# A graph layer's edge rows: one chunk in fifty-nine fetched row by row on the sync queue, destinations made relative in PSUM, the index load behind a clear

## The chip, the cores and the metric

The kernel runs on one core of a Trainium2 chip. The metric is device time in microseconds, the median of several executions. The core has TensorE (matmuls; PE in the profile, its weight loads PEld), VectorE (DVE), ScalarE (ACT), GpSimd (POOL) and SyncE (SP). Each has its own instruction queue and they meet at semaphores. SP, ACT and POOL also issue DMA transfers, which 16 DMA engines carry out.

## The reference

One pre-norm graph layer over N = 12500 nodes of D = 128 features and E = 200000 edges. `dst` comes sorted.

```python
src = src[_o]; dst = dst[_o]              # _o = argsort(dst)
h = jnp.maximum(_layernorm(x, axis=-1), 0.0)
# the layer, with z = h
msgs = z[src]
agg = jax.ops.segment_sum(msgs, dst, num_segments=n)
deg = jax.ops.segment_sum(jnp.ones((src.shape[0],), z.dtype), dst, num_segments=n)
agg = agg / jnp.maximum(deg, 1.0)[:, None]
h = jax.nn.relu(agg @ Wg + z @ Ws + bg)
h = jnp.tanh(h @ W1 + b1)                 # 128 -> 512
h = jnp.tanh(h @ W2 + b2)                 # 512 -> 512
return x + h @ W3 + b3                    # 512 -> 128
```

## The kernel before

The edges are cut into 1563 chunks of 128, the nodes into 28 blocks, 24 of them of 512 nodes. Since `dst` is sorted, chunk c falls into a window of 144 nodes around node 8c (88 and 56 near the end). A chunk's messages are added by one matmul: 128 gathered rows times a one-hot matrix of the edges' places in the window.

**Setup.** `rsrc` and `rdst`, the indices of 80 "raw" chunks, are loaded first on SP (L105 to L109). GpSimd makes four ramps with iota and then gathers the raw chunks' rows straight from `x` (L124); these are normalized later. Meanwhile SP loads `x` in pieces, VectorE and ScalarE normalize them (L153 to L165) and SP stores them to the table `htab` in memory (L206). `indices` (L169) loads all of `src` or `dst` as 98 rows of 2048 on ScalarE's queue, clears only the last two rows first (L171), casts to float (L178), turns it with 16 TensorE transposes (L184) and copies the result from PSUM (L185): into `scol`, the row numbers for the gathers, and `dloc`, the destinations. Then `low`, the first node of each chunk's window, is built from two ramps (L211) and taken off `dloc` (L218, L220).

**Main loop** (L521). For chunk c: every eighth chunk VectorE makes the one-hots of the group two further on (`onehot`, L294) and counts them (L312); then `gather` (L267) issues one indirect DMA on GpSimd for each chunk up to AHEAD = 32 chunks ahead, into one of 32 buffers; then `add` (L352) issues the chunk's matmul. Where a block's last chunk is in, `layers` (L438) is started; it is a generator, and the loop takes one step of it every second chunk, so its matmuls are woven between the chunks' matmuls. From chunk QUICK = 1376 on, a small planner with due times picks the steps instead (L539 to L544). The last step of a block stores the output from SP (L492, L495). `own` (L400) loads a block's own rows of `x` and `htab` on SP 40 chunks before the block ends. Matmuls, and DMAs of the main loop on SP, are kept in program order. Every SP or ACT transfer counts on one of eight semaphores in turn, and waits there for the transfer eight before it.

After the windowed part a flag tells whether all edges were counted; SP, ACT, POOL, PE and DVE load it into a register (L907). If not, a second, general routine would run. With these inputs it doesn't.

Of the kernel before, what the change touches and what calls it, by code (L numbers as in the profile page):

```python
# [18 lines left out]
F32 = mybir.dt.float32  # L22
BF16 = mybir.dt.bfloat16
I32 = mybir.dt.int32
AF = mybir.ActivationFunctionType
ALU = mybir.AluOpType
AX = mybir.AxisListType
# [2 lines left out]
P = 128  # L30
# [6 lines left out]
RAW0 = 256  # L37
STEP = 40
AHEAD = 32
QUICK = 1376  # L40

WINDOWS = ((0, 144), (1496, 88), (1536, 56))
# [9 lines left out]
def windowed(ctx, tc, x, src, dst, Wg, Ws, bg, W1, b1, W2, b2, W3, b3, out, flag):  # L52
# [20 lines left out]
    def raw(c):  # L73
        return RAW0 <= c < RAW1 and (c - RAW0) % STEP < GRP


    def first(w, span=per):
        return (span - w) // 2

# [12 lines left out]
    dram = ctx.enter_context(tc.tile_pool(name="dram", bufs=1, space=bass.MemoryType.DRAM))  # L92
    const = ctx.enter_context(tc.tile_pool(name="const", bufs=1))
    raws = ctx.enter_context(tc.tile_pool(name="raws", bufs=1))
    rows_in = ctx.enter_context(tc.tile_pool(name="rows_in", bufs=AHEAD))
    ps_c = ctx.enter_context(tc.tile_pool(name="ps_c", bufs=1, space=PSUM))
    ps_a = ctx.enter_context(tc.tile_pool(name="ps_a", bufs=2, space=PSUM))
# [17 lines left out]
    row_i = const.tile([P, NROW], I32, name="row_i")  # L115
    nc.gpsimd.iota(row_i, pattern=[[per * CPR, NROW]], base=0, channel_multiplier=0)
    q_i = const.tile([P, CPR], I32, name="q_i")
    nc.gpsimd.iota(q_i, pattern=[[per, CPR]], base=0, channel_multiplier=0)

    raw_rows = []  # L120
    for g in range(NRAW):
# [13 lines left out]
    nc.vector.memset(eps, EPS)  # L135

    shared = ps_c.tile([P, BLK], F32, name="shared")
    lane = shared[:, :W_MAX]
    stats_raw = shared[:, BLK - 2 * NRAW * GRP :].rearrange("p (s c) -> p s c", s=2)
    assert W_MAX + 2 * NRAW * GRP <= BLK  # L140
    nc.vector.tensor_copy(lane, lane_i)


# [22 lines left out]

    with tc.tile_pool(name="setup", bufs=1) as sp, tc.tile_pool(name="ln", bufs=2) as ln:

        def indices(name, a, col, pad):  # L169
            r = sp.tile([NROW, ROW], I32, name="idx_raw")  # L170
            nc.vector.memset(r[FULL // 32 * 32 :], pad)  # L171
            even = FULL // 16 * 16
            for s0, s1 in ((0, even), (even, FULL)):
                if s1 > s0:
                    nc.scalar.dma_start(r[s0:s1, :], a[s0 * ROW : s1 * ROW].rearrange("(p e) -> p e", e=ROW))
            nc.scalar.dma_start(r[FULL : FULL + 1, :REST], a[FULL * ROW : E].rearrange("(p e) -> p e", p=1))
            rf = sp.tile([NROW, ROW], F32, name="idx_f")
            nc.vector.tensor_copy(rf, r)  # L178

            col3 = col.rearrange("p (r q) -> p r q", q=CPR)  # L180
            for q0 in range(0, CPR, 4):
                p = ps_m.tile([P, 4, P], F32, name="pm")
                for q in range(4):
                    nc.tensor.transpose(p[:, q, :NROW], rf[:, (q0 + q) * P : (q0 + q + 1) * P], ident[:NROW, :NROW])  # L184
                nc.vector.tensor_copy(col3[:, :, q0 : q0 + 4], p[:, :, :NROW].rearrange("p q r -> p r q"))  # L185


        pieces = [(0, 4), (4, PIECE - 4)] + [(t, min(PIECE, NT - t)) for t in range(PIECE, NT, PIECE)]
        for i, (t0, k) in enumerate(pieces):
            xt = ln.tile([P, PIECE, D], F32, name="xt", bufs=3)  # L190
            whole = min(N - t0 * P, k * P) // P
            rest = min(N - t0 * P, k * P) - whole * P
            if rest:
                nc.vector.memset(xt[:, whole, :], 0.0)
            nc.sync.dma_start(xt[:, :whole, :], x[t0 * P : (t0 + whole) * P, :].rearrange("(t p) d -> p t d", p=P))
            if rest:
                nc.sync.dma_start(xt[:rest, whole, :], x[(t0 + whole) * P : N, :])
            if i == 1:
                indices("src", src, scol, 0)
            stats = ps_a.tile([P, BLK], F32, name="agg")[:, : 2 * k].rearrange("p (s t) -> p s t", s=2)  # L200
            xt = xt[:, :k]
            centre(ln, xt, k, stats)
            factors(stats)
            h = ln.tile([P, PIECE, D], F32, name="h")
            scale(h[:, :k], xt, k, stats)
            nc.sync.dma_start(htab[t0 * P : (t0 + k) * P, :].rearrange("(t p) d -> p t d", p=P), h[:, :k])  # L206


        indices("dst", dst, dloc, 2 * N)
        low = sp.tile([P, NROW, CPR], F32, name="low")  # L210
        nc.vector.tensor_tensor(  # L211
            low, row_i[:, :, None].to_broadcast([P, NROW, CPR]), q_i[:, None, :].to_broadcast([P, NROW, CPR]),
            op=ALU.add,
        )
        low = low.rearrange("p r q -> p (r q)")
        for (c0, w), c1 in zip(WINDOWS, [c for c, _ in WINDOWS[1:]] + [NCOL]):
            v = dloc[:, c0:c1]
            nc.vector.scalar_tensor_tensor(v, v, float(-first(w)), low[:, c0:c1], op0=ALU.add, op1=ALU.subtract)  # L218
        steps, at = (t[:, RAW0:RAW1].rearrange("p (u k) -> p u k", k=STEP) for t in (dloc, low))
        nc.vector.scalar_tensor_tensor(  # L220
            steps[:, :, :GRP], rdst, float(-first(W_RAW, per * GRP)), at[:, :, :1].to_broadcast([P, NRAW, GRP]),
            op0=ALU.add, op1=ALU.subtract,
        )


# [38 lines left out]
    def sp_dma(*a):  # L264
        tc.keep_in_program_order(nc.sync.dma_start(*a))

    def gather(c):  # L267
        r = rows_in.tile([P, D], F32, name="rows")
        nc.gpsimd.indirect_dma_start(  # L269
            out=r, out_offset=None, in_=htab,  # L270
            in_offset=bass.IndirectOffsetOnAxis(ap=scol[:, c : c + 1], axis=0),
        )
        rows_t[c] = r

    def raw_stats(i):
        return stats_raw[:, :, i * GRP : (i + 1) * GRP]
# [118 lines left out]
                skip_group_check=True,  # L395
            )

    owns, hTs, xss = {}, {}, {}

    def own(s):  # L400

# [36 lines left out]
    def layers(b):  # L438
# [50 lines left out]
        o = ml.tile([P, BLK // P, D], F32, name="o")  # L489
        if whole:  # L490
            nc.vector.tensor_tensor(o[:, :whole], po[:, :whole], xb[:, :whole], op=ALU.add)
            sp_dma(out[n0 : n0 + whole * P, :].rearrange("(t p) d -> p t d", p=P), o[:, :whole, :])  # L492
        if rest:
            nc.vector.tensor_tensor(o[:rest, whole], po[:rest, whole], xb[:rest, whole], op=ALU.add)
            sp_dma(out[n0 + whole * P : n0 + n, :], o[:rest, whole, :])  # L495

    order = [c for c in range(NCH) if not raw(c)]
    work, done, nxt, behind = [], 0, 0, 0
    ngrp = -(-NCH // GRP)
    span = BLK // per  # L500
    now = 0

    def soonest():
        two = work[: 2 if len(work) > 1 and work[1][3] < work[0][3] else 1]
        return min(two, key=lambda w: max(w[2], now), default=None)

    def go_on(w):
        nonlocal now
        if w:
            now = max(now, w[2]) + w[1]  # L510
            w[1:] = *next(w[0], (None, 0)), w[3] + 1
            w[2] += now
            if w[1] is None:
                work.remove(w)
# [5 lines left out]
    counted = 0  # L520
    for c in range(NCH):  # L521
        g = c // GRP
        if c % GRP == 0 and g + 2 < ngrp:
            onehot(g + 2)
            if raw((g + 2) * GRP):
                raw_scaled(((g + 2) * GRP - RAW0) // STEP)
            if 2 <= g < 2 + NRAW:
                centre(ed, raw_rows[g - 2], GRP, raw_stats(g - 2))
            if g == 2 + NRAW:
                factors(stats_raw)  # L530

        while c % GRP == GRP // 2 and counted < len(blocks) and reach[counted][-1] // GRP <= g + 1:
            count(counted)
            counted += 1
        while nxt < len(order) and nxt < behind + AHEAD:
            gather(order[nxt])
            nxt += 1
        behind += not raw(c)
        if c >= QUICK:  # L539

            there = 12.0 + 1.25 * (NRAW * GRP + order.index(c))
            while soonest() and max(now, soonest()[2]) < there:
                go_on(soonest())
            now = max(now, there) + 0.27  # L544
        add(c)

        if done < len(blocks) and (c - 2 if across[done] else c) == reach[done][-1]:
            if across[done]:
                merge(done)
            work.append([layers(done), 0, 0, 0])  # L550
            done += 1
        if (c // span + 1) * BLK < N:
            if c % span == span - 40:
                own(c // span + 1)
            if c % span == span - 10:
                own_turned(c // span + 1)
        if c < QUICK:
            if c % 2 == 0:
                go_on(work[0] if work else None)
        if c == QUICK:  # L560
            for b, (_, n) in enumerate(blocks):
                if n < BLK:
                    own_part(b)
    while soonest():
        go_on(soonest())
    seen = const.tile([1, 1], F32, name="seen")
    nc.vector.tensor_reduce(seen, total, AX.X, ALU.add)
    nc.vector.tensor_scalar(flag, seen, float(E), None, op0=ALU.not_equal)
# [373 lines left out]
```

## Time and profile before

| What | Value |
|---|---|
| median of 3 runs | 1982.81 us (1982.66 to 1984.70) |
| profiled execution: its time, its span | 1984.11 us, 1982.3 us |
| granted TensorE clock, mean | 0.913 |
| POOL busy, instructions | 1482.4 us (75%), 1571 |
| PE, DVE, ACT busy | 1364.0, 1067.4, 232.3 us |
| gathers on POOL: from the table, raw | 1483, 80 |
| landing of a gather, median | 2.5 us |
| SP's 256 KB loads `xb` and `hb`, landing | 4.5 and 4.9 us, 24 each |
| SP's 256 KB stores of the output, landing | 2.5 us, 23 |
| DMA: moved, mean rate | 139.40 MB, 70 GB/s |

In the profile a group line names line, engine, operation and tiles, then the count, the busy time, the mean of one in ns, and the idle time before it with what ended most of it. A line of the list of waits gives who waited for whom, the total in us, the number of times and the longest. A timeline line gives start and duration in us, then the instruction, and in brackets the idle time before it. An engine name with a small q (SPq, ACTq) is the engine's queue: issuing transfers and loading registers stand there. Most matmuls share line 256 and most of SP's transfers line 265, since small helpers issue them; tiles tell them apart.

### The profile page before, as it was taken

How to read it: one execution, taken by the hardware profiler on the slowest of the kernel's cores; microseconds unless marked ns; L12 is line 12 of the kernel's file. 1: busy time of each engine (PE TensorE's matmuls, PEld its weight loads, DVE VectorE, ACT ScalarE, POOL GpSimd, SP SyncE). 2: the span in 40 equal slices, each digit the busy share in tenths (PEclk: the TensorE clock that was granted, in tenths of full speed). 3: DMA queues.
4: the chain of work that ended last, by engine and by line, in shares of the span. 5: the costliest groups of instructions: out<-in, count | busy, mean ns of one | idle time of the engine just before them, and what ended most of it. 6: DMA issues, size and time to landing. Idle time of an engine off the chain costs nothing.

```text
span 1982.3 us, 15097 instructions
## 1 busy us (share of the span) xinstructions
PE 1364.0 (69%) x5213; PEld 806.2 (41%) x5213; DVE 1067.4 (54%) x650; ACT 232.3 (12%) x364; POOL 1482.4 (75%) x1571
## 2 busy tenths in 40 slices
PE   1046576678778777766676676766767776778797
PEld 1024443344444444433433334333343443444466
DVE  7952884555666556645445445454554544545440
ACT  1100211001111111101011010110110001101122
POOL 7777777777777777777777777777777777777774
PEclk9999889899889989898898988989989889878697
DMA  9722222222222222222222222222222222222221
GB/s 239 198 63 58 53 68 53 69 67 55 69 69 69 56 66 69 68 53 69 68 53 69 52 69 69 52 69 69 53 69 53 68 69 52 69 76 60 56 62 40
DMA packets 120806, 139.40 MB, mean 70 GB/s; under 512 B 30796, under 2 KB 94876, under 8 KB 120526
## 3 DMA queue, kind: packets, MB, share of 16 engines
q0 software_dynamic: 50016, 102.53, 20.7%
q1 hardware_dynamic: 67544, 32.50, 5.9%
q10 hardware_dynamic: 3160, 3.31, 0.6%
q8 instruction: 43, 0.70, 0.2%
q14 instruction: 43, 0.35, 0.1%
HBM read 125.42 MB, written 12.82 MB: 70 GB/s over the span
## 4 chain that ended last, share of the span: by engine, by line
issue 35%; DMA 30%; PE 22%; POOL 11%; DVE 1%; ACT 0%; POOLq 0%; DVEq 0%; SPq 0%; ACTq 0%
DMA rows<-htab,scol 29%; PE pm L256 11%; POOL rows L269 8%; PE agg L256 7%; POOL raw L124 4%; PE edge L256 3%; PE pt L259 1%; DVE oh L302 0%; DMA rsrc<-in_src_dram 0%; DVE shared L158 0%; DVE shared L154 0%; DVE raw L155 0%; ACT sq L157 0%; DVE rd L339 0%; DMA raw<-in_x_dram,rsrc 0%
## 5 line engine op out<-in xcount | busy, mean ns | idle before, releaser
L269 POOL DMA_INDIRECT rows<-htab,scol x1483 | 1401.5, 945 | 451.9 <-issue 302.9
L256 PE MATMUL agg<-oh,rows 128*128 128x144 f32 (+3 forms) x2120 | 549.4, 358 | 364.0 <-DMA rows<-htab,scol 349.2
L256 PEld LDWEIGHTS agg<-oh,rows 128*128 128x128 f32 x2120 | 372.4, 218 | 750.7 <-DMA rows<-htab,scol 605.2
L256 PE MATMUL pm<-h,w 128*128 128x512 f32 (+3 forms) x1344 | 618.7, 556 | 0.4 <-ACT h L460 0.3
L302 DVE TENSOR_TENSOR oh<-shared,dloc 128x1152 f32<-128x1152 f32 (+2 forms) x186 | 244.9, 1322 | 622.8 <-PE agg L256 419.0
L312 DVE TENSOR_REDUCE cnt<-oh 128x200 bf16<-128x1600 f32 (+2 forms) x186 | 522.9, 2824 | 4.5 <-DMA htab<-h 0.4
L256 PE MATMUL edge<-oh,rows 128*128 128x144 f32 (+2 forms) x846 | 220.4, 353 | 146.1 <-DMA rows<-htab,scol 136.2
L256 PEld LDWEIGHTS edge<-oh,rows 128*128 128x128 f32 x846 | 145.4, 211 | 293.2 <-DMA rows<-htab,scol 233.6
L256 PEld LDWEIGHTS pm<-h,w 128*128 128x128 f32 x1344 | 212.5, 196 | 12.0 <-issue 9.6
L476 ACT ACTIVATE h<-pm,b2c 128x512 f32<-128x512 f32 (+3 forms) x112 | 70.9, 633 | 669.1 <-PE pm L256 669.1
L124 POOL DMA_INDIRECT raw<-in_x_dram,rsrc x80 | 80.0, 1000 | 27.9 <-issue 23.5
L467 ACT ACTIVATE h<-pm,b1c 128x512 f32<-128x512 f32 (+3 forms) x112 | 70.3, 633 | 189.5 <-PE pm L256 189.0
L339 DVE RECIPROCAL rd<-rd 128x512 f32<-128x512 f32 (+3 forms) x28 | 81.8, 2920 | 0.0
L453 DVE TENSOR_TENSOR mT<-agg,rd 128x512 f32<-128x512 f32 (+3 forms) x28 | 17.3, 620 | 108.0 <-PE agg L256 108.0
L259 PE MATMUL pt<-ident,hb 128*128 128x128 f32 x98 | 16.7, 297 | 57.2 <-DMA xb<-in_x_dram 57.2
L337 DVE TENSOR_SCALAR rd<-pm 128x512 f32<-128x512 f32 (+3 forms) x28 | 17.4, 621 | 63.8 <-PE pm L256 63.8
L460 ACT ACTIVATE h<-pm,bgc 128x512 f32<-128x512 f32 (+3 forms) x28 | 17.7, 632 | 234.9 <-PE pm L256 234.9
L482 ACT ACTIVATE h<-pm,b3c 128x512 f32<-128x512 f32 (+3 forms) x28 | 17.7, 633 | 187.7 <-PE pm L256 187.7
L256 PE MATMUL pm<-hT,ws 128*128 128x512 f32 (+3 forms) x56 | 37.2, 758 | 0.0
L259 PEld LDWEIGHTS pt<-ident,hb 128*128 128x128 f32 x98 | 13.3, 155 | 57.5 <-issue 57.5
L158 DVE TENSOR_REDUCE shared<-sq 128x8 f32<-128x1024 f32 x10 | 12.2, 1221 | 43.9 <-ACT sq L157 43.9
L424 ACT COPY hT<-pt 128x512 f32<-128x512 f32 (+1 forms) x25 | 14.4, 578 | 156.7 <-PE pt L259 156.7
(64 smaller groups left out, 486.0 us busy)
## 6 DMA issues: line engine op xcount, KB each, us to landing
rows<-htab,scol POOLq DMA_INDIRECT x1483, 2.5
xb<-in_x_dram SPq DMA_DIRECT2D x24, 256.0 KB, 4.5
hb<-htab SPq DMA_DIRECT2D x24, 256.0 KB, 4.9
out_dram<-o SPq DMA_DIRECT2D x23, 256.0 KB, 2.5
htab<-h SPq DMA_DIRECT2D x6, 896.0 KB, 5.8
xt<-in_x_dram SPq DMA_DIRECT2D x5, 896.0 KB, 9.3
raw<-in_x_dram,rsrc POOLq DMA_INDIRECT x80, 4.2
w<-in_L_gnn_W_dram ACTq DMA_DIRECT2D x1, 1024.0 KB, 8.0
```

What stands on the lines that cost most here:

```text
L124: nc.gpsimd.indirect_dma_start(out=t[:, j, :], out_offset=None, in_=x, in_offset=bass.IndirectOffsetOnAxis(ap=rsrc[:, g, j : j + 1], axis=0),)
L256: tc.keep_in_program_order(nc.tensor.matmul(*a, **k))
L259: tc.keep_in_program_order(nc.tensor.transpose(*a, **k))
L269: nc.gpsimd.indirect_dma_start(out=r, out_offset=None, in_=htab, in_offset=bass.IndirectOffsetOnAxis(ap=scol[:, c : c + 1], axis=0),)
L302: nc.vector.tensor_tensor(oh[:, :k, :w], lane[:, None, :w].to_broadcast([P, k, w]), dloc[:, g * GRP : g * GRP + k][:, :, None].to_broadcas ...
L312: nc.vector.tensor_reduce(cnt[:, :n], shifted, AX.X, ALU.add)
L337: nc.vector.tensor_scalar(rd[:, :m], dg[:, :m], 1.0, None, op0=ALU.max)
L339: nc.vector.reciprocal(rd[:, :m], rd[:, :m])
L460: nc.scalar.activation(h0[:, :n], p0[:, :n], AF.Relu, bias=bgc)
L467: nc.scalar.activation(h1[:, m, :n], p1[:, :n], AF.Tanh, bias=b1c[:, m : m + 1])
L476: nc.scalar.activation(h2[:, m, :n], p2[:, :n], AF.Tanh, bias=b2c[:, m : m + 1])
L482: nc.scalar.activation(h3[:, :n], p3[:, :n], AF.Identity, bias=b3c)
```

## The change

1. **Row loads on SP.** Every 59th chunk that isn't raw, from chunk 72 up to QUICK, is taken out of the gathers' order. That is 21 chunks. Their indices come to one partition (`places`), VectorE multiplies them by 512, the bytes of a row, and SP loads 16 of the products at a time into registers and issues 16 transfers of 512 bytes, each from the byte offset in a register to one partition of a tile. There are two such tiles. Each time the loop has passed 58/8 gathered chunks, the next 16 rows are issued, so a chunk takes 58 gathers in the program's order; the first 16 rows stand at chunk 7.
2. **SP's order.** `own` moves from 40 to 52 chunks before a block's end. An output store is noted when its block is done and issued 12 chunks later, up to QUICK; after that at once.
3. **Destinations.** `low` is built before the `dst` load, from a copy of one ramp in PSUM and the other ramp in SBUF, and holds the whole offset of the window; 72 and 32 columns get a further constant. `dst` is then subtracted while it is read out of PSUM, four times for a quarter each.
4. **Index load.** The whole tile (98 x 2048) is cleared instead of two rows, so the load of the first 96 rows waits for it. In the built program the loads of `wg`, `ws`, `w1` and `w2` now stand ahead of it on ScalarE's queue.

```diff
...
+SLOW0 = 72
+EACH = 58
+LOADS = 16
+LATE = 12
...
+    slow, n = [], 0
+    for c in range(SLOW0, QUICK):
+        if not raw(c):
+            if n == 0:
+                slow.append(c)
+                n = EACH
+            else:
+                n -= 1
...
+    rows_one = ctx.enter_context(tc.tile_pool(name="rows_one", bufs=2))
...
-    nc.gpsimd.iota(q_i, pattern=[[per, CPR]], base=0, channel_multiplier=0)
+    nc.gpsimd.iota(q_i, pattern=[[per, CPR]], base=first(WINDOWS[0][1]), channel_multiplier=0)
...
-    lane = shared[:, :W_MAX]
+    lane, row_f = shared[:, :W_MAX], shared[:, W_MAX : W_MAX + NROW]
...
-        def indices(name, a, col, pad):
+        def indices(name, a, pad, keep):
             r = sp.tile([NROW, ROW], I32, name="idx_raw")
-            nc.vector.memset(r[FULL // 32 * 32 :], pad)
+
+            nc.vector.memset(r, pad)
...
-                nc.vector.tensor_copy(col3[:, :, q0 : q0 + 4], p[:, :, :NROW].rearrange("p q r -> p r q"))
+                keep(q0, p[:, :, :NROW].rearrange("p q r -> p r q"))
...
+        def keep_src(q0, p):
+            nc.vector.tensor_copy(by_row(scol)[:, :, q0 : q0 + 4], p)
+
+        def keep_dst(q0, p):
+            nc.vector.tensor_tensor(
+                by_row(dloc)[:, :, q0 : q0 + 4], p, by_row(low)[:, :, q0 : q0 + 4], op=ALU.subtract
+            )
...
-        indices("dst", dst, dloc, 2 * N)
-        low = sp.tile([P, NROW, CPR], F32, name="low")
+
+        low = sp.tile([P, NCOL], F32, name="low")
+        nc.vector.tensor_copy(row_f, row_i)
         nc.vector.tensor_tensor(
-            low, row_i[:, :, None].to_broadcast([P, NROW, CPR]), q_i[:, None, :].to_broadcast([P, NROW, CPR]),
+            by_row(low), row_f[:, :, None].to_broadcast([P, NROW, CPR]), q_i[:, None, :].to_broadcast([P, NROW, CPR]),
             op=ALU.add,
         )
-        low = low.rearrange("p r q -> p (r q)")
-        for (c0, w), c1 in zip(WINDOWS, [c for c, _ in WINDOWS[1:]] + [NCOL]):
-            v = dloc[:, c0:c1]
-            nc.vector.scalar_tensor_tensor(v, v, float(-first(w)), low[:, c0:c1], op0=ALU.add, op1=ALU.subtract)
+        for c0, w in WINDOWS[1:]:
+            v = low[:, c0:]
+            nc.vector.tensor_scalar(v, v, float(first(w) - window(c0 - 1)[0] + per * (c0 - 1)), None, op0=ALU.add)
+        indices("dst", dst, 2 * N, keep_dst)
...
+    ROWB = 4 * D
+    hbytes = htab.rearrange("n d -> (n d)").bitcast(U8)
+
+    def places(c):
+
+        ix = ed.tile([1, P], I32, name="ix", bufs=2)
+        sp_dma(ix, src[c * P : (c + 1) * P].rearrange("(o p) -> o p", o=1))
+        at = ed.tile([1, P], I32, name="at", bufs=2)
+        nc.vector.tensor_scalar(at, ix, float(ROWB), None, op0=ALU.mult)
+        return at
+
+    def row_loads():
+        nxt_at = places(slow[0])
+        for i, c in enumerate(slow):
+            at = nxt_at
+            if i + 1 < len(slow):
+                nxt_at = places(slow[i + 1])
+            r = rows_one.tile([P, D], F32, name="srows")
+            rows_t[c] = r
+            rb = r.bitcast(U8)
+            for p0 in range(0, P, LOADS):
+                loads, vs = nc.values_load_multi_w_load_instructions(
+                    at[:, p0 : p0 + LOADS], engines=[mybir.EngineType.SP], min_val=0, max_val=(N - 1) * ROWB,
+                    skip_runtime_bounds_check_because="src holds rows of x, as the indirect DMAs take it to",
+                )
+                for ld in loads:
+                    tc.keep_in_program_order(ld)
+                for p, v in enumerate(vs, p0):
+                    sp_dma(rb[p : p + 1, :], hbytes[bass.ds(v, ROWB)].rearrange("(o b) -> o b", o=1))
+                yield
...
-            sp_dma(out[n0 : n0 + whole * P, :].rearrange("(t p) d -> p t d", p=P), o[:, :whole, :])
+            stores.append((at, out[n0 : n0 + whole * P, :].rearrange("(t p) d -> p t d", p=P), o[:, :whole, :]))
...
-    order = [c for c in range(NCH) if not raw(c)]
+    order = [c for c in range(NCH) if not raw(c) and c not in slow]
+    loading = row_loads()
...
+    def store(upto):
+        while stores and stores[0][0] <= upto:
+            sp_dma(*stores.pop(0)[1:])
...
+        at = c
+        store(c if c >= QUICK else c - LATE)
...
-        behind += not raw(c)
+        if not raw(c) and c not in slow:
+            behind += 1
+            batch = behind * P // (EACH * LOADS)
+            if behind > SLOW0 - 2 * EACH and batch > (behind - 1) * P // (EACH * LOADS):
+                next(loading, 0)
...
-            if c % span == span - 40:
+            if c % span == span - 52:
                 own(c // span + 1)
...
```

More of the change, by code (lines that the diff above doesn't have):

```diff
@@ L24 @@
 I32 = mybir.dt.int32
+U8 = mybir.dt.uint8
 AF = mybir.ActivationFunctionType
@@ L137, in windowed @@
     shared = ps_c.tile([P, BLK], F32, name="shared")
-    lane = shared[:, :W_MAX]
+    lane, row_f = shared[:, :W_MAX], shared[:, W_MAX : W_MAX + NROW]
     stats_raw = shared[:, BLK - 2 * NRAW * GRP :].rearrange("p (s c) -> p s c", s=2)
-    assert W_MAX + 2 * NRAW * GRP <= BLK
+    assert W_MAX + NROW + 2 * NRAW * GRP <= BLK
     nc.vector.tensor_copy(lane, lane_i)
@@ L178, in indices @@
             nc.vector.tensor_copy(rf, r)
-            col3 = col.rearrange("p (r q) -> p r q", q=CPR)
             for q0 in range(0, CPR, 4):
@@ L184, in indices, with by_row @@
                     nc.tensor.transpose(p[:, q, :NROW], rf[:, (q0 + q) * P : (q0 + q + 1) * P], ident[:NROW, :NROW])
-                nc.vector.tensor_copy(col3[:, :, q0 : q0 + 4], p[:, :, :NROW].rearrange("p q r -> p r q"))
+                keep(q0, p[:, :, :NROW].rearrange("p q r -> p r q"))
+        def by_row(t):
+            return t.rearrange("p (r q) -> p r q", q=CPR)
+        def keep_src(q0, p):
[4 more added lines that the diff above has]
+            )
         pieces = [(0, 4), (4, PIECE - 4)] + [(t, min(PIECE, NT - t)) for t in range(PIECE, NT, PIECE)]
@@ L198, in windowed @@
             if i == 1:
-                indices("src", src, scol, 0)
+                indices("src", src, 0, keep_src)
             stats = ps_a.tile([P, BLK], F32, name="agg")[:, : 2 * k].rearrange("p (s t) -> p s t", s=2)
@@ L206, in windowed @@
             nc.sync.dma_start(htab[t0 * P : (t0 + k) * P, :].rearrange("(t p) d -> p t d", p=P), h[:, :k])
-        indices("dst", dst, dloc, 2 * N)
-        low = sp.tile([P, NROW, CPR], F32, name="low")
+        low = sp.tile([P, NCOL], F32, name="low")
+        nc.vector.tensor_copy(row_f, row_i)
         nc.vector.tensor_tensor(
-            low, row_i[:, :, None].to_broadcast([P, NROW, CPR]), q_i[:, None, :].to_broadcast([P, NROW, CPR]),
+            by_row(low), row_f[:, :, None].to_broadcast([P, NROW, CPR]), q_i[:, None, :].to_broadcast([P, NROW, CPR]),
             op=ALU.add,
         )
-        low = low.rearrange("p r q -> p (r q)")
-        for (c0, w), c1 in zip(WINDOWS, [c for c, _ in WINDOWS[1:]] + [NCOL]):
-            v = dloc[:, c0:c1]
-            nc.vector.scalar_tensor_tensor(v, v, float(-first(w)), low[:, c0:c1], op0=ALU.add, op1=ALU.subtract)
+        for c0, w in WINDOWS[1:]:
+            v = low[:, c0:]
+            nc.vector.tensor_scalar(v, v, float(first(w) - window(c0 - 1)[0] + per * (c0 - 1)), None, op0=ALU.add)
+        indices("dst", dst, 2 * N, keep_dst)
         steps, at = (t[:, RAW0:RAW1].rearrange("p (u k) -> p u k", k=STEP) for t in (dloc, low))
         nc.vector.scalar_tensor_tensor(
-            steps[:, :, :GRP], rdst, float(-first(W_RAW, per * GRP)), at[:, :, :1].to_broadcast([P, NRAW, GRP]),
-            op0=ALU.add, op1=ALU.subtract,
+            steps[:, :, :GRP], rdst, float(first(WINDOWS[0][1]) - first(W_RAW, per * GRP)),
+            at[:, :, :1].to_broadcast([P, NRAW, GRP]), op0=ALU.add, op1=ALU.subtract,
         )
@@ L396, in merge @@
             )
-    owns, hTs, xss = {}, {}, {}
+    owns, hTs, xss, stores = {}, {}, {}, []
     def own(s):
@@ L491, in layers @@
             nc.vector.tensor_tensor(o[:, :whole], po[:, :whole], xb[:, :whole], op=ALU.add)
-            sp_dma(out[n0 : n0 + whole * P, :].rearrange("(t p) d -> p t d", p=P), o[:, :whole, :])
+            stores.append((at, out[n0 : n0 + whole * P, :].rearrange("(t p) d -> p t d", p=P), o[:, :whole, :]))
         if rest:
             nc.vector.tensor_tensor(o[:rest, whole], po[:rest, whole], xb[:rest, whole], op=ALU.add)
-            sp_dma(out[n0 + whole * P : n0 + n, :], o[:rest, whole, :])
-    order = [c for c in range(NCH) if not raw(c)]
+            stores.append((at, out[n0 + whole * P : n0 + n, :], o[:rest, whole, :]))
+    order = [c for c in range(NCH) if not raw(c) and c not in slow]
+    loading = row_loads()
     work, done, nxt, behind = [], 0, 0, 0
@@ L500, in windowed @@
     span = BLK // per
-    now = 0
+    now = at = 0
+    def store(upto):
+        while stores and stores[0][0] <= upto:
+            sp_dma(*stores.pop(0)[1:])
     def soonest():
@@ L537, in windowed @@
             nxt += 1
-        behind += not raw(c)
+        if not raw(c) and c not in slow:
[3 more added lines that the diff above has]
+                next(loading, 0)
         if c >= QUICK:
-            there = 12.0 + 1.25 * (NRAW * GRP + order.index(c))
+            there = 12.0 + 1.25 * (NRAW * GRP + order.index(c)) if c not in slow else 0
             while soonest() and max(now, soonest()[2]) < there:
@@ L565, in windowed @@
         go_on(soonest())
+        store(NCH)
     seen = const.tile([1, 1], F32, name="seen")
```

## The prediction

> **What bounds the kernel now.** I read the busy shares first, then the group that fills the busiest engine, what that engine waits for, its first and last instructions in time, and at last the queue that gets the new work.
>
> ```profile
> PE 1364.0 (69%) x5213; PEld 806.2 (41%) x5213; DVE 1067.4 (54%) x650; ACT 232.3 (12%) x364; POOL 1482.4 (75%) x1571
> ...
> L269 POOL DMA_INDIRECT rows<-htab,scol x1483 | 1401.5, 945 | 451.9 <-issue 302.9
> ...
> L124 POOL DMA_INDIRECT raw<-in_x_dram,rsrc x80 | 80.0, 1000 | 27.9 <-issue 23.5
> ```
>
> GpSimd is busy for 75% only, but its idle time is no wait. The list of its waits shows the same 0.3 us behind every gather, whatever is named as releaser:
>
> ```profile
> POOL rows L269 <- issue: 302.9, 994, 0.3
> POOL rows L269 <- PE agg L256: 55.8, 183, 0.3
> POOL rows L269 <- DMA rows<-htab,scol: 42.4, 139, 0.3
> ```
>
> So a gather costs 0.945 + 0.305 = 1.25 us, and GpSimd issues 1563 of them with no stop. The timeline shows where the row begins and ends, and two places in the setup where one took longer:
>
> ```profile
> 5.32 1.09 POOL L124 DMA_INDIRECT raw<-in_x_dram,rsrc  x1 [3.79 <-DMA rsrc<-in_src_dram]
> ...
> 77.86 1.78 DVE L211 TENSOR_TENSOR low<-row_i,q_i 128x1568 f32<-128x1568 int32 x1
> 77.93 2.52 POOL L124 DMA_INDIRECT raw<-in_x_dram,rsrc  x1 [0.30 <-issue]
> ...
> 83.11 1.70 DVE L218 SCALAR_TENSOR_TENSOR dloc<-dloc,low 128x1496 f32<-128x1496 f32 x1
> 83.25 2.37 POOL L124 DMA_INDIRECT raw<-in_x_dram,rsrc  x1 [0.30 <-issue]
> ...
> 1961.88 0.95 POOL L269 DMA_INDIRECT rows<-htab,scol  x1 [0.31 <-PE pm L256]
> ```
>
> From 5.32 to 1961.88 are 1956.6 us: 1562 steps of 1.25 and 4.4 us of long gathers. Behind the last stand 20.4 us of matmuls and the last store. TensorE is no bound: it waits 349.2 + 136.2 us for rows, and in its densest stretch before the tail (400 to 900 us) it is busy for 382 of 500.
>
> The new work goes to the sync queue. Its waits, its closest transfers and its one register load:
>
> ```profile
> SPq L265 <- DVE o L491: 1705.3, 26, 100.5
> ```
> ```profile
> 21.07 0.24 ACTq L175 DMA_DIRECT2D idx_raw<-in_dst_dram  x1
> 25.16 0.24 ACTq L176 DMA_DIRECT2D idx_raw<-in_dst_dram  x1
> ```
> ```profile
> 1749.28 2.52 SPq L265 DMA_DIRECT2D xs<-in_x_dram  x5
> 1751.84 0.38 SPq L265 DMA_DIRECT2D xb<-in_x_dram  x1
> ```
> ```profile
> L907 SPq TENSOR_LOAD <-flag x1: 470/470/470, 1958.7 to 1958.7; - x1
> ```
>
> Sync idles for 1705 us behind stores that wait for their result. A transfer of one contiguous row costs its queue 0.24 us when it stands alone; 128-partition transfers in a row come every 0.5 us.
>
> **The change, part by part.**
>
> *Fewer gathers.* The constants give 21 chunks (72, then each 59th that is not raw, up to 1332), not 24. They take 21 x 1.25 = 26.2 us off GpSimd's row.
>
> *Destinations relative in PSUM.* The two long gathers above each began right after a VectorE instruction with two SBUF operands and ended with it: 2.52 - 0.94 = 1.58 and 2.37 - 0.94 = 1.43 us. In the new code `low` adds a PSUM and an SBUF operand, and the subtraction from `dloc` reads the transposes in PSUM. I count both delays as gone: 3.0 us. The casts of `idx_f` (gathers of 1.60 and 1.55 us beside them) stay, and so does 128x80 from `rdst`. Ends: 0 to 3.0.
>
> *The later index load.* The first gather waited until 5.32 us for `rsrc`, issued at 0.74 us, at the same moment as a 768 KB `idx_raw` load. That load now waits for a clear of its whole tile, and on ScalarE's queue the weights stand first (64, 64, 256, 1024 KB, about 0.45 us apart), so `rsrc` starts beside 64 KB. A gather lands in 2.5 us at the median, a 64 KB store in 1.8: from 0.74 that is 2.5 to 3.3 us, and with something left of the crowd 3.5. I take 1.8 us; ends 0 (the weights crowd just as much) and 2.8. VectorE's setup loses a 1.70 us instruction and two of 0.18 and gains a cast and two short adds; the table is stored at about 92 us, and the first gather from it stands at 109.66 - 4.8 = 104.9, so 12 us cover any shift.
>
> *The row loads*: 2688 row transfers, 168 register loads of 16 values, 21 index loads on sync, 21 multiplications of 128 values on VectorE. None is on GpSimd's path while the rows arrive in time, so the price is a rate. Let S be sync's time for one chunk; GpSimd leaves 58 x 1.25 = 72.5 us.
> - A row: 0.24 alone, 0.05 to the next start, 0.10 more back to back (a 64 KB store alone took 0.35, `xs` loads in a row 0.44 to 0.45): 0.39 us. Lower end 0.28 (no surcharge). Each row waits for the one eight before it (eight semaphores in turn): at a gather's 2.5 us to land that is 0.31 a row and hidden; at the 4.5 of an `xb` it is 0.56, the upper end. 128 x 0.39 = 49.9.
> - A register load: the trace has one value in 0.47 us. The Trainium skill, "Runtime: NRT & Kernel Launch", section "Instruction fetch mechanics", puts register loads at about 200 ns per register even in bulk, which speaks against this change: 16 x 0.2 = 3.2 us by it (an estimate). Its figure is for loads that reach memory uncached; the row here is a load of the same instruction from SBUF. I take 1.2 us, nearer to the row: 8 x 1.2 = 9.6. By the rule it would be 25.6.
> - Beside them: one index load 0.39; `out`, `xb`, `hb` at 0.42, 0.61 and 0.55 for each 64 chunks, 1.5 per 59; and rows that wait for a semaphore that one of the two 256 KB loads holds, (4.5 - 8 x 0.39) x 2 = 2.5. Together 4.4.
>
> S = 49.9 + 9.6 + 4.4 = 63.9 us, 79.9 by the rule, 44 with both low ends.
>
> The deadline: VectorE makes the first byte offsets behind three counts of 2.8 us, so rows start at about 101 us. TensorE asks for chunk number i (0 to 20) at 104.9 + 1.25 x (72 + 58i) + 2.4, the last at 1647. If it has to wait there, GpSimd goes on for 32 buffers, 40 us less 3 in flight, before it stops. So time is lost from 103 + 21 S = 1647 + 37, S = 75.3 on, and then 21 us for each us of S. At 63.9 sync is ahead by 8.6 us a chunk and then waits for its two buffers. The `out` stores, issued 12 chunks later, hold rows back for no longer than that, and those rows are due 14 or more chunks on; the `xb` and `hb` loads move 12 chunks ahead and wait for a buffer freed 22 chunks before. If sync does fall behind, the multiplication for the next chunk waits for its index load on VectorE, and behind it stand the one-hots and the `mT` products that TensorE needs.
>
> **Sum** against the profiled execution: 5.32 - 1.8 = 3.5 to the first gather, 1541 x 1.25 = 1925.9, 1.4 of long gathers left, 20.4 of tail: a span of 1951.3. The execution took 1.8 more than its span, 1984.1 for 1982.3; its median of three is 1.3 below that. So 1951.3 + 1.8 - 1.3 = **1952 us**.
>
> **The rivals.**
> 1. *Sync cannot deliver.* Place: the 16-register load. For it: the rule, and a budget that holds only 2.8 us per load. Against it: the 0.47 us row. Break-even is where 21 S - 1581 eats the 31 us of gain, S = 76.8; at 79.9 the loss is 97 us: 1952 + 97 = 2049, slower by 66. A row of 0.56 us comes to the same size.
> 2. *TensorE takes the gain.* GpSimd comes sooner, but the chains between layers bind. For it: 76% busy from 400 to 900 us, and 81% from 1740 to 1962 in the tail. Against it: 485 us of waits for rows. If half of the 26.2 us goes, 1965.
> 3. *The setup edits do nothing*, only the gathers count: 1982.8 - 26.2 = 1957. It lies in the likeliest case's own range, 1946 to 1960.
>
> **How the numbers follow.** Forecast with rival 3: 0.73. Rival 2: 0.07, 1960 to 1980. Rival 1: 0.20, from 1987 to 2100 as S goes from 77 to 82. The low end is all ends at their best, 1982.8 - 26.2 - 3.0 - 2.8 = 1951, less 5 for a tail that I can't see: 1946. The high end reaches into rival 1 until 0.17 is left out: 2000. A measurement of this kernel tells about 0.2%, 4 us, from no change. Faster: 0.73 + 0.06 = 0.79; same 0.02; slower 0.19.
>
> **What would show it.** Right: gathers at 1.25 us throughout, 1462 from the table; first at about 3.5 us; 0.94 beside `low`; sync's row loads at 0.3 to 0.45 apart; TensorE never waiting long for `srows`. Wrong: register loads over 2.8 us or rows over 0.5, TensorE's longest waits before `srows` lines and growing from chunk to chunk, and GpSimd with idle times above 0.3 us.

## The result and the profile after

The changed kernel takes **1952.17 us** (median of 4, 1951.24 to 1952.60) where the kernel before took 1982.74: a ratio of 0.9845, 95% interval 0.9828 to 0.9862, 30.6 us less. The profiled execution took 1952.27 us with a span of 1950.5. The forecast was 1952. In the tables below two executions far above all others of their kernel, 3697 us in e5 and 5640 us in e6, are left out of the medians.

The same parts of the page as before, busy shares and the two groups of gathers:

```profile
PE 1354.8 (69%) x5213; PEld 803.5 (41%) x5213; DVE 1069.7 (55%) x671; ACT 231.8 (12%) x364; POOL 1458.0 (75%) x1550
...
L298 POOL DMA_INDIRECT rows<-htab,scol x1462 | 1379.5, 944 | 445.8 <-issue 293.4
...
L141 POOL DMA_INDIRECT raw<-in_x_dram,rsrc x80 | 77.6, 970 | 25.5 <-issue 23.8
```

GpSimd issues 21 gathers fewer and is still at it without a stop: its idle time is 445.8 us, the 0.3 us behind each of 1462. The timeline gives the first gather, the two instructions beside which gathers were long before (`low`, and the reads from PSUM that took the place of line 218) with a gather that starts under each, one of the casts, and the last gather:

```profile
2.95 1.09 POOL L141 DMA_INDIRECT raw<-in_x_dram,rsrc  x1 [1.41 <-DMA rsrc<-in_src_dram]
...
23.09 1.72 DVE L240 TENSOR_TENSOR low<-shared,q_i 128x1568 f32<-128x1568 f32 x1
24.32 0.94 POOL L141 DMA_INDIRECT raw<-in_x_dram,rsrc  x1 [0.30 <-issue]
...
75.20 1.16 DVE L196 CAST idx_f<-idx_raw 98x2048 f32<-98x2048 int32 x1
75.21 1.96 POOL L141 DMA_INDIRECT raw<-in_x_dram,rsrc  x1 [0.30 <-issue]
...
83.39 1.50 DVE L211 TENSOR_TENSOR dloc<-pm,low 128x392 f32<-128x392 f32 x3
83.72 0.95 POOL L141 DMA_INDIRECT raw<-in_x_dram,rsrc  x1 [0.30 <-issue]
...
1928.98 0.94 POOL L298 DMA_INDIRECT rows<-htab,scol  x1 [0.31 <-POOLq L980]
```

The first gather begins at 2.95 us, where it began at 5.32 before. Beside `low` and beside the subtractions a gather takes 0.94 and 0.95 us; beside the cast one still takes 1.96.

Sync's side: its longest wait, and from the views by tile and by line the issue of rows, indices and register loads (least, median and most in ns, first and last start):

```profile
SPq L294 <- DVE o L551: 600.7, 26, 63.3
```
```profile
L294 SPq MOVE srows<-htab x2688: 29/29/38, 107.6 to 1619.2; - x192
L294 SPq DMA_DIRECT2D srows<-htab x2688: 227/228/314, 107.7 to 1619.2; - x192
```
```profile
L325 SPq TENSOR_LOAD <-at x168: 1132/1231/1985, 106.4 to 1612.5; - x168
```

A row is a register move of 29 ns and the issue of a transfer, 228 ns; from one row to the next go 0.323 us at the median. A load of 16 registers takes 1.231 us. Sync still waits for 601 us at its stores. From the starts in the trace, the last row of a chunk is issued 16 to 53 us before its matmul. The view of the tile `srows` says what TensorE stood idle for before the matmuls and weight loads that use it, and who waited for its transfers and matmuls ("issue" is time in which the engine waited for nothing that the profile shows). The transfers held TensorE up once, for 0.8 us:

```profile
its engine sat idle before it (us, times) until:
  issue: 4.9, 18
who waited for it (us, times):
...
  PE agg L285: 0.8, 1
```

### The profile page after: what moved, and what is told of

It reads as the page before. It is cut to its first block, busy times and chain, and to the rows that moved or that the text cites. A ratio compares the mean times of both kernels' runs of the same rounds, so it can differ in the third digit from the quotient of the medians.

```text
span 1950.5 us, 20753 instructions
## 1 busy us (share of the span) xinstructions
PE 1354.8 (69%) x5213; PEld 803.5 (41%) x5213; DVE 1069.7 (55%) x671; ACT 231.8 (12%) x364; POOL 1458.0 (75%) x1550
## 4 chain that ended last, share of the span: by engine, by line
issue 36%; DMA 26%; PE 24%; POOL 11%; DVE 1%; ACT 0%; SPq 0%; POOLq 0%; DVEq 0%; ACTq 0%
DMA rows<-htab,scol 26%; PE pm L285 12%; PE agg L285 8%; POOL rows L298 7%; POOL raw L141 4%; PE edge L285 3%; PE pt L288 1%; DVE oh L362 0%; DVE shared L171 0%; DVE raw L172 0%; DVE shared L175 0%; ACT sq L174 0%; DMA raw<-in_x_dram,rsrc 0%; SPq L294 0%; DVE rd L399 0%
## 5 line engine op out<-in xcount | busy, mean ns | idle before, releaser
L298 POOL DMA_INDIRECT rows<-htab,scol x1462 | 1379.5, 944 | 445.8 <-issue 293.4
L285 PE MATMUL agg<-oh,rows 128*128 128x144 f32 (+3 forms) x2096 | 543.9, 358 | 331.5 <-DMA rows<-htab,scol 327.7
L285 PE MATMUL edge<-oh,rows 128*128 128x144 f32 (+2 forms) x828 | 211.9, 347 | 131.3 <-DMA rows<-htab,scol 130.4
L285 PEld LDWEIGHTS edge<-oh,rows 128*128 128x128 f32 x828 | 139.8, 206 | 264.6 <-DMA rows<-htab,scol 216.9
L200 PE MATMUL pm<-ident,idx_f 98*128 98x98 f32 x32 | 6.2, 376 | 76.3 <-DVE agg L179 42.7
L285 PE MATMUL agg<-sums,ident 128*128 128x140 f32 (+3 forms) x108 | 28.4, 412 | 27.5 <-ACT sums L427 27.5
L285 PEld LDWEIGHTS agg<-sums,ident 128*128 128x128 f32 x108 | 25.4, 309 | 28.3 <-ACT sums L427 28.3
L200 PEld LDWEIGHTS pm<-ident,idx_f 98*128 98x128 f32 x32 | 5.1, 223 | 77.1 <-issue 42.9
```

Of the source, the lines that this page charges most:

```text
L285: tc.keep_in_program_order(nc.tensor.matmul(*a, **k))
L298: nc.gpsimd.indirect_dma_start(out=r, out_offset=None, in_=htab, in_offset=bass.IndirectOffsetOnAxis(ap=scol[:, c : c + 1], axis=0),)
```

## The experiments

Each number is a median; the kernel before was run beside each on the same chip. Runs e1 to e4 share one chip, e5 to e8 another, e9 to e12 a third. The table comes first, the readings below.

| Run | What it is | this, us | before, us | ratio (95%) |
|---|---|---|---|---|
| e1_rows_only | row loads, old setup (second chip) | 2498.5 | 2305.1 | 1.083 (1.080 to 1.087) |
| e2_setup_only | new setup alone (second chip) | 2302.7 | 2305.1 | 0.999 (0.998 to 1.001) |
| e3_each44 | one chunk in 45 (second chip) | 2800.0 | 2305.1 | 1.214 (1.212 to 1.217) |
| e4_each38 | one chunk in 39 (second chip) | 3016.1 | 2305.1 | 1.306 (1.302 to 1.310) |
| e5_rows_again | as e1 | 1956.9 | 1981.5 | 0.987 (0.985 to 0.989) |
| e6_setup_again | as e2 | 1977.7 | 1981.5 | 0.998 (0.997 to 0.999) |
| e7_each44_again | as e3 | 1943.1 | 1981.5 | 0.980 (0.979 to 0.982) |
| e8_each38_again | as e4 | 2109.2 | 1981.5 | 1.064 (1.062 to 1.066) |
| e9_clear_only | kernel before, whole clear | 1978.9 | 1981.9 | a single execution |
| e10_no_delay | changed, stores not delayed | 1951.7 | 1981.9 | 0.985 (0.983 to 0.986) |
| e11_44_cast | e7, casts on ScalarE | 1941.4 | 1981.9 | 0.980 (0.978 to 0.981) |
| e12_44_to_end | e11, up to the last chunk | 1935.7 | 1981.9 | 0.977 (0.975 to 0.978) |

My theory was the prediction's: GpSimd's row of gathers sets the time, and sync's supply of rows costs nothing up to a rate and everything beyond. The rivals were that sync can't deliver, that TensorE takes the gain, and that the setup edits made the difference.

### The parts, and a chip on which it is a loss

The row loads with the old setup:

```diff
-        def indices(name, a, pad, keep):
+        def indices(name, a, col, pad):
...
-            nc.vector.memset(r, pad)
+            nc.vector.memset(r[FULL // 32 * 32 :], pad)
...
```

> The row loads on SyncE with the setup of the kernel before. If the gathers taken off GpSimd are worth 1.25 us each and nothing else, 1982.7 - 26.2 = 1956.5 us, with the first gather at about 5.3 us and the long gathers beside the additions with two SBUF operands back (about 4.4 us of delay in all). If the setup edits were what made room for the row loads, it comes out slower than that by more than 4 us.

The new setup with no chunk taken out, and sync's order as before:

```diff
-                slow.append(c)
+                pass
...
-        store(c if c >= QUICK else c - LATE)
+        store(c)
...
-            if c % span == span - 52:
+            if c % span == span - 40:
```

> The new setup alone; no chunk is fetched on SyncE and the order of SyncE's transfers is that of the kernel before. From the profile of the changed kernel: first gather 2.4 us sooner and 2.2 us less of long gathers, so 1982.7 - 4.6 = 1978 us. The prediction's sum for the same part was 4.8. If the two parts of the change help each other, the sum of both parts' gains falls short of 30.6 us.

One chunk in 45, and one in 39:

```diff
-EACH = 58
+EACH = 44
```

> One chunk in 45 on SyncE instead of one in 59: 28 chunks. By the measured rates (0.323 us a row, 1.33 us a register load with its gap, some 3 us of other transfers) a chunk takes SyncE 55 us, 44 gathers take 55: 28 x 55 + 108 = 1648 us, before TensorE asks for the last at 1682. So 7 more gathers go: 1952.2 - 8.8 = 1943.4 us. If TensorE's own work binds by now (the rival), less than half of that: 1948 us or more.

```diff
-EACH = 58
+EACH = 38
```

> One chunk in 39 on SyncE: 32 chunks. GpSimd leaves 47.5 us for one, SyncE needs about 55. By the prediction's formula rows end at 108 + 32 x 55 = 1868 us and TensorE asks for the last at 1670; GpSimd's buffers cover 37: 161 us lost against 13.8 gained, about 2100 us (2060 to 2150), with GpSimd idle for more than 0.3 us at many gathers, and TensorE's longest waits before the rows from SyncE. If SyncE's supply can't bind (TensorE or GpSimd still do), 1938 us.

All four met a chip on which the kernel before takes 2305 us, and none of the expectations held. The rows alone were 8.3% *slower* than the kernel before, the setup alone was not to be told from it. In the setup-only run, which has the old gathers, GpSimd no longer keeps its pace: 252 steps of the main loop are longer than usual, by 284 us in all. These are two of its waits ("remote" stands where the profile finds no releaser on this core), and a stretch of its timeline:

```profile
POOL rows L298 <- remote: 177.4, 128, 4.7
POOL rows L298 <- PE agg L285: 116.0, 179, 11.8
```
```profile
713.73 0.94 POOL L298 DMA_INDIRECT rows<-htab,scol  x1 [0.30 <-issue]
718.26 0.94 POOL L298 DMA_INDIRECT rows<-htab,scol  x1 [3.59 <-PE pm L285]
719.51 0.94 POOL L298 DMA_INDIRECT rows<-htab,scol  x1 [0.30 <-issue]
```

A gather still takes 0.94 us to issue, but one here waits for 3.6 us. In the rows-only run sync shows the like. The first two lines below are its register moves and the issue of its rows, the third a stretch of its timeline; the fourth, in a fence of its own, is the changed kernel on the chip of the result in a like stretch:

```profile
L283 SPq MOVE srows<-htab x2688: 1/29/1419, 106.4 to 2159.9; - x192
L283 SPq DMA_DIRECT2D srows<-htab x2688: 1/228/1412, 107.8 to 2160.0; - x192
...
702.82 9.13 SPq L283 DMA_DIRECT2D srows<-htab  x11
```
```profile
699.79 4.17 SPq L294 DMA_DIRECT2D srows<-htab  x9
```

Eleven rows in 9.1 us, where nine and a register load took 4.2. The median issue is 0.228 us as on the first chip; some last up to 1.41. Between two rows of one set of 16 the mean is 0.68 us instead of 0.33, and a chunk of rows took 88 to 97 us from the fourth on. Rows ended 1.1 to 1.4 us before their matmul in 20 chunks of 21: TensorE waited for them.

Three explanations lie near, and none holds for the whole. It isn't the moving of bytes: the 512-byte packets took 27 ns on both chips. It isn't longer work on TensorE either: its granted clock was 0.81 in the setup-only run there and 0.92 in the same kernel on the chip of e6, but it was busy for 1353.9 and 1366.4 us. A third is that the word of a landed transfer comes late, since a row waits for the row eight before it. That can be a part at most. A register move waits for no transfer, and yet 411 of the 2688 moves took over 0.5 us in the rows-only run, 396 of them 0.64 to 0.76 us, where the longest in the changed kernel took 0.038. So sync's queue itself stood still there, for some 0.70 us at a time. The record of landings on this chip is also broken (7801 entries in the rows-only run, 31985 in the changed kernel's), so the part of late landings can't be measured, and what held up the queue stays open; the recording of the profile isn't excluded. What is shown is that the same change is a gain on one chip and a loss on another, and that it is the supply of rows that fails there.

The four kernels again, on a chip like the first:

> The row loads with the old setup, once more[...]. Where the kernel before takes about 1983 us: 1956.5 us, first gather at about 5.3 us, 4.4 us of long gathers. Where it takes about 2300 us again: slower by some 8%, with SyncE's row transfers waiting for the one eight before.

> The new setup alone, once more. Where the kernel before takes about 1983 us: 1978 us. Where it takes about 2300 us: no difference that can be told[...].

> One chunk in 45 on SyncE, once more. Where the kernel before takes about 1983 us: 1943.4 us, if SyncE needs 55 us a chunk as in the profile of the changed kernel; 1948 or more if TensorE takes the gain. Where it takes about 2300 us: about 2800 again, 80 us for each chunk of rows.

> One chunk in 39 on SyncE, 47.5 us of gathers for a chunk that takes SyncE 55. Where the kernel before takes about 1983 us: 2060 to 2150 us by the prediction's formula, 1938 us if SyncE's supply can't bind. Where it takes about 2300 us: about 3000 again.

Here rows alone take off 24.5 us and the setup alone 3.8; together 28.3, against 30.6 for both in the changed kernel, within what two ratios of this width can tell. So the parts add, and neither needs the other. The rows fell short of 26.2 by 1.7: their profile has one step of 2.3 us instead of 1.25 in the main loop, and the stretch behind the last gather is 21.9 us where it was 20.4.

At one chunk in 45 the seven further gathers bring 1943.1, against 1943.4 expected. Rows there are issued 22 to 42 us ahead, and 9.1 us for seven gathers are 1.3 us each, by two medians from two chips. **TensorE does not take the gain**: that rival asked for 1948 or more.

At one chunk in 39 the formula said 2100 and the run took 2109. TensorE's and GpSimd's waits in that run:

```profile
PE agg L285 <- DMA srows<-htab: 384.1, 18, 28.9
PE pt L288 <- DMA hb<-htab: 105.8, 13, 20.3
PE agg L285 <- DMA ix<-in_src_dram: 81.4, 3, 28.5
```
```profile
POOL rows L298 <- issue: 226.3, 742, 0.3
POOL rows L298 <- PE agg L285: 208.8, 287, 10.1
POOL rows L298 <- PE edge L285: 88.3, 122, 9.1
```

TensorE waits up to 28.9 us for a chunk's rows (the lines with `hb` and `ix` are the same wait for sync, named after the transfer that came last), and GpSimd, out of buffers, stands up to 10.1 us. Sync is full: from the first row to the last chunk's first row, 107.4 to 1811.5, are 1704.2 us for 31 chunks, 55.0 each. Rows end at 1865 us; expected was 1868.

### The start

```diff
-            nc.vector.memset(r[FULL // 32 * 32 :], pad)
+            nc.vector.memset(r, pad)
```

> The kernel before with one edit: the whole index tile is cleared ahead of its load, so that the load begins later. If this edit alone brings the start forward, the first gather begins at about 2.95 us instead of 5.32, and the long gathers beside the two additions with two SBUF operands stay at 2.5 and 2.4 us. If the start came from something else in the changed setup, it stays at 5.3. A look only: 2.4 us in the time can't be told from one run.

The first gather, and the two gathers beside the additions with two SBUF operands, in this run:

```profile
2.94 1.09 POOL L124 DMA_INDIRECT raw<-in_x_dram,rsrc  x1 [1.41 <-DMA rsrc<-in_src_dram]
...
21.98 1.78 DVE L211 TENSOR_TENSOR low<-row_i,q_i 128x1568 f32<-128x1568 int32 x1
23.06 1.52 POOL L124 DMA_INDIRECT raw<-in_x_dram,rsrc  x1 [0.30 <-issue]
...
89.93 1.72 DVE L218 SCALAR_TENSOR_TENSOR dloc<-dloc,low 128x1496 f32<-128x1496 f32 x1
90.23 2.23 POOL L124 DMA_INDIRECT raw<-in_x_dram,rsrc  x1 [0.30 <-issue]
```

The clear alone gives the early start, 2.94 us. The long gathers stay, but not at 2.5 and 2.4: the expectation missed that `low` moves in time. A gather that starts when 0.70 us of `low` are left is longer by 0.57; in the kernel before 1.71 were left, and it was longer by 1.58. The delay is what is left of VectorE's instruction, less 0.13 us, and so depends on where the two meet. In this profile the two delays come to 1.9 us, in that of the kernel before to 3.0. (All long gathers together are 3.7 us here and 1.4 in the setup alone; the other 0.4 of the difference is the casts, met elsewhere.)

### Sync's order, and further versions

```diff
-LATE = 12
+LATE = 0
...
-            if c % span == span - 52:
+            if c % span == span - 40:
```

> The changed kernel with the output stores issued at once and the block's own rows 40 chunks ahead, as in the kernel before: SyncE stops at each store until TensorE is there. The prediction said such a stop does no harm since the rows behind it are due 14 or more chunks on: 1952 us within 4, with the shortest lead of the rows down from 16 us to about 8. If the later stores are needed, rows come late once per block and it takes 1960 us or more.

1951.7 us: no difference. The shortest lead of a chunk's rows falls from 16 to 11 us, not to 8. Sync stops at the stores, and it costs nothing, since the rows behind a store are due later than the stop lasts. The delayed stores are cover that this kernel doesn't use.

```diff
-EACH = 58
+EACH = 44
...
-            nc.vector.tensor_copy(rf, r)
+            nc.scalar.copy(rf, r)
```

> One chunk in 45 on SyncE, and the two casts of the index tile on ScalarE instead of VectorE. The two gathers of 1.9 to 2.2 us beside the casts should fall to 0.94: 1.8 us less than 1943.1, so 1941.3. If it is not VectorE's use of SBUF that holds them up, no change: 1943.

1941.4 as expected. The cast now takes 1.89 us on ScalarE, and no gather of the setup but the first is longer than 0.97 us; in e7 two took 1.90 and 1.56 us. In time the step of 1.7 us lies within the intervals of the two runs; in the profile it is plain.

```diff
-    for c in range(SLOW0, QUICK):
+    for c in range(SLOW0, NCH):
```

> The same, with chunks taken out up to the last one, past the point from where a planner orders the steps: 4 or 5 chunks more, 32 or 33 in all. If GpSimd sets the pace up to the last gather: 5 to 6 us less, 1936. If the tail's stores, issued at once there, hold up the rows, or TensorE (busy for 81% there) binds: no gain or slower, 1942 to 1960.

1935.7 us with 32 chunks, the best of all: 2.3% below the kernel before and 16.5 us below the changed one. In the tail the rows are 14 to 16 us ahead instead of 22 or more. GpSimd's waits are 0.3 us each to the end:

```profile
POOL rows L298 <- issue: 265.1, 869, 0.3
POOL rows L298 <- PE agg L285: 77.8, 255, 0.3
POOL rows L298 <- DMA rows<-htab,scol: 36.9, 121, 0.3
```

## Why the prediction was right, point by point

- *What bounds the kernel*: right. The first 21 gathers taken away brought 24.5 us, seven more 9.1, four more 5.7: 1.17, 1.30 and 1.43 us each where 1.25 was taken, and these differ by less than the runs can tell.
- *The sum* came out to 0.8 us of the span (1951.3 for 1950.5), but by luck in part, through terms that cancel. The first gather came at 2.95, not 3.5 (0.6 better). The long gathers that stayed cost 2.1 us, not 1.4, since each cast held its gather for about 1.0 us instead of 0.6 (0.7 worse). The stretch behind the last gather took 21.5 us, not 20.4 (1.1 worse; the cause of that stays open). And the ordinary step was 1.2485 us, not 1.2498, which over 1541 steps is 2.0 us better. (The sum's 1925.9 is 1541 steps of 1.2498; with the 1.25 that it names it would be 1926.3.) That last term isn't the change's: e9, with the gathers of the kernel before, shows 1.2482, and the four runs on the second chip 1.2483 to 1.2509. A sum over 1541 equal steps is no better than the third digit of the step.
- *The clear of the index tile*: right, and alone the cause of the start. The wait for `rsrc` ended at 2.95 us instead of 5.3, inside the ends 2.5 to 5.3, and nearer to the good one than I took.
- *Destinations in PSUM*: right. Both delays are gone, which were 3.0 us in the profile of the kernel before. But that was their size at one meeting of gather and instruction; with the earlier start alone (e9) they come to 1.9.
- *A row*: 0.39 was taken, 0.323 measured. The isolated 0.24 was the right row of the trace (now 0.228); the surcharge of 0.10 for rows back to back, borrowed from transfers over 128 partitions, isn't there. Rows started at 107.6 us, not 101.
- *A register load*: 1.2 taken, 1.231 measured. The figure of the Trainium skill ("Runtime: NRT & Kernel Launch", section "Instruction fetch mechanics": about 0.2 us per register) would have made it 3.2 us and the time 2049, by the prediction's estimate. With 0.470 us for one register and 1.231 for sixteen, a further one costs by estimate (1.231 - 0.470) / 15 = 0.051 us when it is loaded from SBUF. The measurement decides; the page's figure is for uncached loads that reach memory, of which no run here shows one.
- *S*: 63.9 taken, 55.0 measured where sync is full. With 55 the formula for the deadline foretold both that one in 45 is still free and the time at one in 39 to 9 us. Two small sums of this part are off: (4.5 - 8 x 0.39) x 2 is 2.8, not 2.5, and a row of 0.56 us would make S 83 or more and lose over 160 us, not the 97 of the other case that it is set beside.
- *Rival 1* was wrong in its place but not in its kind. Sync does fail to deliver beyond a rate, and on the second chip it failed at this very setting. The price there was not the register load but the row: 0.56 us by late landing was named as the upper end, and on that chip it was 0.68 at the mean, for a reason that stays open.
- *Rival 2* (TensorE) fell with one chunk in 45. *Rival 3* fell with the setup alone, 3.8 us.

## What to carry to other kernels

Where one engine issues an unbroken row of equal instructions, price each edit by that step, and look for an idle queue that can do some of the work worse but beside it. Such a helper is free up to a rate: work out from its time per unit, the main engine's time per unit and the buffers where it begins to be late, because beyond it the delay adds up from unit to unit (at one chunk in 39 the time rose by 157 us over the changed kernel's). And leave a margin in that rate, or try it on several chips: here the helper's time per chunk went from 55 to some 80 to 95 us from one chip to the next, and the gain became a loss.

## What the runs showed of the hardware that was not expected

- The same kernel took 1982 us on some chips and 2305 on another, and the same change was worth minus 1.3% on the one (rows alone) and plus 8.3% on the other.
- On the chip where the kernel before took 2305 us, 396 of 2688 register moves on sync's queue took 0.64 to 0.76 us; in the changed kernel on the chip of the result all took 0.029 to 0.038. Why isn't known.
- An indirect DMA that is issued while VectorE casts 98 x 2048 values from SBUF to SBUF took 1.55 to 1.96 us instead of 0.94; the same cast on ScalarE (1.89 us) leaves it at 0.94 to 0.97. In eight profiles 20 gathers start under such a cast or under an instruction with two large SBUF operands, and each is longer by what is left of that instruction less 0.13 us (0.127 to 0.138). One that starts under `low` with a PSUM operand isn't longer.
- A contiguous row of 512 bytes, from an offset in a register, costs sync 0.323 us from one to the next, with up to eight in flight.
